# Bilinear field pairs: a third weight tile, field 0 in the weight ring, and stores of four pairs instead of three

## The chip, the cores and the metric

One core of a Trainium2 chip runs the kernel. The metric is device time in microseconds (us) of one execution. The kernel before took 762.01 us (median of three runs, 761.2 to 763.02). The profiled execution took 760.73 us, of which its trace spans 758.7 us from the first to the last instruction. The granted TensorE clock was 0.985 on the mean.

## The reference

There are 32 fields. Each has a vector of 128 numbers for each of 1024 examples. For every pair of fields (i, j) with i < j, 496 pairs in all, the vector of field i goes through that pair's own 128x128 matrix and is then multiplied, element by element, with the vector of field j:

```python
I_IDX, J_IDX = all (i, j) with i < j          # 496 pairs
v_i = inputs[:, I_IDX, :]                     # 1024 x 496 x 128, float32
v_j = inputs[:, J_IDX, :]
transformed = jnp.einsum('bpd,ped->bpe', v_i, W)   # W: 496 x 128 x 128
return transformed * v_j                      # 1024 x 496 x 128, float32
```

The inputs are 16.8 MB of fields and 32.5 MB of matrices; the output is 260 MB. That the output is five times the input is what shapes this kernel.

## The kernel before

**Layout.** The 128 output features lie on the 128 partitions, the 1024 examples along the free axis. One pair of one example set is thus a tile of 128 x 1024 float32: 4 KB in each partition, 512 KB in all. A pair is worked in two halves of 512 examples; `u` counts these halves (0 to 991) and `q = u // 2` counts pairs. The pairs are taken from the last row of i to the first: i = 30 has one pair, i = 0 has 31 (q = 465 to 495), so a field is needed as i for the first time long after the kernel began.

**Arithmetic of a half.** The first 15 pairs (`nq0`) multiply the raw float32 matrix with the raw field (L159). All later ones use a split: ScalarE makes a rounded high part `wh` of two matrices (L95), GpSimd makes `wl` and `wd` from it (L96 to L98); a field is split in the same way into `xh`, `xl`, `xd` (L110 to L116, some of the last step on VectorE, L203). TensorE then does two matmuls into a PSUM bank (L162), ScalarE scales the bank in place (L163), TensorE adds a third (L171), and VectorE multiplies the bank with field j into the output tile `ot` (L177). `first(u)` does the first part, `second(u - LAG)` the rest, three halves later.

**Order.** The schedule is manual: each engine works in the order in which the loop at L186 writes its instructions down. ScalarE's order also holds the issues of most loads, and SyncE's order holds the stores.

**Loads of weights.** Eight matrices come at a time (`WL`, 512 KB, rows of 4 KB). The tiles come from a ring `rpool` of `WB` = 2 tiles. `w_at` (L142 to L145) says after which pair the load of tile c is issued: q = 8c - 11, that is six pairs ahead of the first split that reads it (q = 8c - 5), and not before the matrices that lay in that ring tile were used.

**Loads of fields.** `load_x` (L72) gives each of the 32 fields a tile of its own, 4 KB in each partition, that stays to the end, because a field serves as j for many pairs. Field 0 is the exception: it is never a j, so its raw values are read by its own split and by nothing else. The loop issues field i - 7 at the first pair of row i.

**Stores.** The output tiles come from a ring `opool` of four tiles of `OG` = 3 pairs (12 KB in each partition). Once three pairs are in a tile, SyncE issues one store of 1.5 MB with rows of 12 KB (L184). The first group and the last pairs go one by one or in halves (L182, L179). A tile can be filled again only when all of its store has landed.

**Start.** SyncE issues weights 0, fields 29 and 28, weights 1 and fields 27 to 24; ScalarE issues fields 30 and 31.

Of the kernel before, what the change touches and what calls it, by code (L numbers as in the profile page):

```python
# [7 lines left out]
F32 = mybir.dt.float32  # L8
# [3 lines left out]
P = 128  # L12
NF = 32
NQ = NF * (NF - 1) // 2
BT = 1024
HB = 512
WC = 2
WL = 8
OG = 3
EPS = 2.0**-12  # L20
NATIVE = 5
SHARED = 10
XDLAG = 10
LAG = 3
WB = 2
WLEAD = 6
XLEAD = 5


def _pairs():  # L30

    return [(i, j) for i in range(NF - 2, -1, -1) for j in range(i + 1, NF)]


@with_exitstack
def kernel(
    ctx: ExitStack,
    tc: tile.TileContext,
    xt: bass.AP,
    wt: bass.AP,  # L40
    out: bass.AP,
):

    nc = tc.nc
    pairs = _pairs()  # L60
    nchunk = NQ // WC

    xpool = ctx.enter_context(tc.tile_pool(name="x", bufs=1))
    spool = ctx.enter_context(tc.tile_pool(name="xs", bufs=2))
    rpool = ctx.enter_context(tc.tile_pool(name="wr", bufs=WB))
    wpool = ctx.enter_context(tc.tile_pool(name="ws", bufs=4))
    opool = ctx.enter_context(tc.tile_pool(name="o", bufs=4))
    ppool = ctx.enter_context(tc.tile_pool(name="ps", bufs=8, space=bass.MemoryType.PSUM))

    x_sb = {}  # L70

    def load_x(f, n=1, pieces=1, eng=None):  # L72

        t = xpool.tile([P, n, BT], F32, tag=f"x{f}", name=f"x_{f}")
        s = BT // pieces
        for k in range(pieces):
            (eng or nc.sync).dma_start(out=t[:, :, k * s : (k + 1) * s], in_=xt[:, f : f + n, k * s : (k + 1) * s])
        for k in range(n):
            x_sb[f + k] = t[:, k, :]

    w_raw = {}

    def load_w(c, splits=(0, WL), eng=nc.scalar):
        w_raw[c] = rpool.tile([P, WL, P], F32, tag="w", name=f"w_{c}")
        for a, b in zip(splits, splits[1:]):
            eng.dma_start(out=w_raw[c][:, a:b, :], in_=wt[c, :, a:b, :])

    w_s = {}

    def split_w(c, u):  # L90

        k = c * WC % WL
        raw = w_raw[c * WC // WL][:, k : k + WC, :].rearrange("p q e -> p (q e)")
        h, l, d = [wpool.tile([P, WC * P], F32R, tag=t, name=f"{t}_{c}") for t in ("wh", "wl", "wd")]
        nc.scalar.mul(h, raw, 1.0 - 2.0**-13)  # L95
        nc.gpsimd.tensor_tensor(l, raw, h.bitcast(F32), ALU.subtract)  # L96
        nc.gpsimd.tensor_scalar(d, h.bitcast(F32), EPS, 1.0, ALU.mult, ALU.mult)  # L97
        nc.gpsimd.tensor_tensor(d, l.bitcast(F32), d.bitcast(F32), ALU.subtract)  # L98
        w_s[c] = (h, l, d)

    x_s = {}
    later = []

    def split_x(f, a, u):

        if a == 0:
            x_s[f] = [spool.tile([P, BT], F32R, tag=t, name=f"{t}_{f}") for t in ("xh", "xl", "xd")]
        s = slice(a, a + HB)
        h, l, d = [t[:, s] for t in x_s[f]]
        nc.scalar.mul(h, x_sb[f][:, s], 1.0 - 2.0**-13)  # L110
        nc.gpsimd.tensor_tensor(l, x_sb[f][:, s], h.bitcast(F32), ALU.subtract)  # L111
        nc.gpsimd.tensor_scalar(l, l.bitcast(F32), 1.0 / EPS, 1.0, ALU.mult, ALU.mult)  # L112
        if f > NF - 2 - NATIVE - SHARED:
            later.append((min(u + XDLAG, 2 * first_q[f] + LAG - 1), d, h.bitcast(F32), l.bitcast(F32)))
        else:
            nc.gpsimd.tensor_tensor(d, h.bitcast(F32), l.bitcast(F32), ALU.subtract)  # L116

    nq0 = NATIVE * (NATIVE + 1) // 2
    c0 = nq0 // WC
    first_q = {i: q for q, (i, j) in reversed(list(enumerate(pairs)))}  # L120

    todo = []
    for c in range(c0, nchunk):
        todo.append(((c - 3) * WC + 1, max(c * WC, nq0), lambda u, c=c: split_w(c, u)))
    for i in range(NF - 2 - NATIVE, -1, -1):
        for a in range(0, BT, HB):
            todo.append((first_q[i + 1] + 1 if i < NF - 3 - NATIVE else 2, first_q[i], lambda u, i=i, a=a: split_x(i, a, u)))
    todo.sort(key=lambda t: t[1])  # L130

    load_w(0, (0, 1, WL), nc.sync)
    load_x(NF - 2, pieces=2, eng=nc.scalar)
    load_x(NF - 1, pieces=2, eng=nc.scalar)
    load_x(NF - 3)
    load_x(NF - 4)
    load_w(1, eng=nc.sync)
    for f in range(NF - 5, NF - 4 - XLEAD, -1):
        load_x(f)


    w_at = {}  # L142
    for c in range(WB, -(-NQ // WL)):
        free = (c - WB + 1) * WL if (c - WB) * WL < nq0 else 0
        w_at[max(c * WL - 3 * WC + 1 - WLEAD, free)] = c  # L145


    ctx.enter_context(tc.manual_schedule())
    po, ots = {}, {}


    def first(u):
        q, h = divmod(u, 2)
        i, c = pairs[q][0], q // WC
        r = slice(q % WC * P, (q % WC + 1) * P)
        s = slice(h * HB, (h + 1) * HB)
        po[u] = ppool.tile([P, HB], F32, tag="po", name=f"po_{u}")
        if q < nq0:
            nc.tensor.matmul(po[u], w_raw[q // WL][:, q % WL, :], x_sb[i][:, s], start=True, stop=True)  # L159
        else:  # L160
            for t in (0, 1):
                nc.tensor.matmul(po[u], w_s[c][t][:, r], x_s[i][t][:, s], start=t == 0, stop=t == 1)  # L162
            nc.scalar.mul(po[u], po[u], 1.0 + EPS)  # L163

    def second(u):
        q, h = divmod(u, 2)
        i, j = pairs[q]
        r = slice(q % WC * P, (q % WC + 1) * P)
        s = slice(h * HB, (h + 1) * HB)
        if q >= nq0:  # L170
            nc.tensor.matmul(  # L171
                po[u], w_s[q // WC][2][:, r], x_s[i][2][:, s], start=False, stop=True, skip_group_check=True
            )
        g, k = divmod(q, OG)
        if k == 0 and h == 0:
            ots[g] = opool.tile([P, OG, BT], F32, tag="ot", name=f"ot_{g}")
        nc.vector.tensor_tensor(ots[g][:, k, s], po.pop(u), x_sb[j][:, s], ALU.mult)  # L177
        if q >= NQ - 2:
            nc.sync.dma_start(out=out[g, :, k, s], in_=ots[g][:, k, s])  # L179
        elif g == 0 or q >= NQ - 1 - OG:  # L180
            if h == 1:
                nc.sync.dma_start(out=out[g, :, k], in_=ots[g][:, k])  # L182
        elif k == OG - 1 and h == 1:
            nc.sync.dma_start(out=out[g], in_=ots[g])  # L184

    for u in range(2 * NQ + LAG):  # L186
        q = u // 2
        if u < 2 * NQ:
            i, j = pairs[q]
            if u % 2 == 0 and j == i + 1 and 0 <= i - 2 - XLEAD:  # L190
                load_x(i - 2 - XLEAD, eng=nc.scalar)
            first(u)
            if u % 2 == 1 and q in w_at:
                load_w(w_at[q])
        if u >= LAG:
            second(u - LAG)
        if u % 2 == 1:
            ready = [t for t in todo if t[0] <= q]
            if ready:
                ready[0][2](u)  # L200
                todo.remove(ready[0])
        while later and later[0][0] <= u:
            nc.vector.tensor_tensor(*later.pop(0)[1:], ALU.subtract)  # L203
    assert not todo and not later
# [27 lines left out]
```

## Time and profile before

| What | Value |
|---|---|
| Time, median of 3 runs | 762.01 us |
| Span of the trace | 758.7 us |
| Bytes moved by DMA | 310.07 MB, 409 GB/s over the span |
| of these, HBM written / read | 260.05 / 49.28 MB |
| PE, DVE, ACT, POOL busy | 93%, 84%, 82%, 78% |
| TensorE clock granted, mean | 0.985 |

The engines named are PE (TensorE, matmuls), PEld (its weight loads), DVE (VectorE), ACT (ScalarE), POOL (GpSimd) and SP (SyncE, which issues the stores). "Busy" is the share of the span in which an engine worked. The DMA figures of the profile count packets: one packet is one contiguous row that one of the core's 16 DMA engines moves, or the 4-byte update of a semaphore with which each of the 16 engines ends its part of a transfer. Queue q1 holds what SyncE issued, q10 what ScalarE issued; q8 and q14 carry the program itself.

### The profile page before, as it was taken

The page shows a single profiled execution, that of the slowest core. Times are in us where ns is not written, and L with a number is a line of the kernel's source. Part 1 is how long each engine was busy: PE and PEld are TensorE (multiplying, and loading weights), DVE is VectorE, ACT ScalarE, POOL GpSimd, SP SyncE. Part 2 cuts the span into 40 slices and gives each one's busy share as a digit, 9 for nine tenths or more (in the row PEclk, how much of TensorE's full clock was granted, in tenths as well). Part 3 has the DMA queues.
Part 4 walks back from the last instruction along what each step waited for, and adds up shares of the span by engine and source line. Part 5 has one row for each costly group of instructions (what it writes and reads, how often), then busy time and mean ns, then how long its engine had stood idle before and what let it go on. Part 6 is the DMA issues. An engine that isn't in the chain of part 4 may idle for free.

```text
span 758.7 us, 11264 instructions
## 1 busy us (share of the span) xinstructions
PE 708.1 (93%) x2946; PEld 551.6 (73%) x2946; DVE 633.7 (84%) x1012; ACT 625.7 (82%) x1256; POOL 595.6 (78%) x863
## 2 busy tenths in 40 slices
PE   7979989999999999999998989999999999999992
PEld 3557778777777777777786878778787777777771
DVE  4869989987888779788797989888888888888883
ACT  1368889988888888888887979898899899989881
POOL 0959999999888987978878787888887878786650
PEclk9999999999999999999999999999999999999996
DMA  9999999999999999999999999999999999999996
GB/s 351 427 406 389 425 394 424 427 418 430 420 422 418 425 423 409 419 416 411 400 411 420 404 423 402 422 417 409 410 414 417 402 423 400 408 424 404 416 412 257
DMA packets 38800, 310.07 MB, mean 409 GB/s; under 512 B 4304, under 2 KB 4432, under 8 KB 17872
## 3 DMA queue, kind: packets, MB, share of 16 engines
q1 hardware_dynamic: 26064, 264.25, 83.1%
q10 hardware_dynamic: 12672, 45.09, 16.0%
q8 instruction: 24, 0.39, 0.2%
q14 instruction: 40, 0.33, 0.1%
HBM read 49.28 MB, written 260.05 MB: 408 GB/s over the span
## 4 chain that ended last, share of the span: by engine, by line
DMA 40%; PE 39%; DVE 12%; POOL 5%; issue 1%; ACT 1%; DVEq 0%; ACTq 0%; POOLq 0%
DMA out_dram<-ot 34%; PE po L162 24%; DVE ot L177 12%; PE po L171 12%; DMA w<-in_wt_dram 6%; PE po L159 4%; POOL xl L111 1%; POOL xd L116 1%; POOL wl L96 1%; POOL xl L112 1%; POOL wd L98 1%; ACT po L163 0%; DMA x<-in_xt_dram 0%; DVE xd L203 0%; POOL wd L97 0%
## 5 line engine op out<-in xcount | busy, mean ns | idle before, releaser
L177 DVE TENSOR_TENSOR ot<-po,x 128x512 f32<-128x512 f32 x992 | 619.8, 683 | 109.4 <-DMA out_dram<-ot 46.6
L163 ACT ACTIVATE po<-po 128x512 f32<-128x512 f32 x962 | 540.7, 582 | 58.6 <-PE po L162 24.4
L162 PE MATMUL po<-xh,wh 128*128 128x512 f32 x962 | 382.6, 398 | 13.6 <-DVE ot L177 12.9
L171 PE MATMUL po<-xd,wd 128*128 128x512 f32 x962 | 377.8, 393 | 12.6 <-ACT po L163 11.4
L162 PE MATMUL po<-xl,wl 128*128 128x512 f32 x962 | 378.7, 394 | 5.6 <-POOL wl L96 5.3
L96 POOL TENSOR_TENSOR wl<-w,wh 128x256 fp32r<-128x256 f32 x241 | 181.0, 751 | 76.0 <-ACT wh L95 62.2
L162 PEld LDWEIGHTS po<-xh,wh 128*128 128x128 f32 x962 | 181.8, 189 | 72.0 <-DVE ot L177 33.9
L171 PEld LDWEIGHTS po<-xd,wd 128*128 128x128 f32 x962 | 181.7, 189 | 54.0 <-POOL wd L97 5.7
L162 PEld LDWEIGHTS po<-xl,wl 128*128 128x128 f32 x962 | 182.0, 189 | 46.3 <-POOL wl L96 9.7
L98 POOL TENSOR_TENSOR wd<-wl,wd 128x256 fp32r<-128x256 f32 x241 | 178.4, 740 | 20.1
L95 ACT ACTIVATE wh<-w 128x256 fp32r<-128x256 f32 x241 | 99.8, 415 | 42.3 <-DMA w<-in_wt_dram 38.7
L97 POOL TENSOR_SCALAR wd<-wh 128x256 fp32r<-128x256 f32 x241 | 99.3, 412 | 20.3
L111 POOL TENSOR_TENSOR xl<-x,xh 128x512 fp32r<-128x512 f32 x52 | 69.2, 1331 | 18.6 <-ACT xh L110 18.3
L116 POOL TENSOR_TENSOR xd<-xh,xl 128x512 fp32r<-128x512 f32 x32 | 41.3, 1291 | 2.7
L110 ACT ACTIVATE xh<-x 128x512 fp32r<-128x512 f32 x52 | 32.6, 631 | 12.6 <-DMA x<-in_xt_dram 12.6
L112 POOL TENSOR_SCALAR xl<-xl 128x512 fp32r<-128x512 f32 x52 | 33.3, 641 | 4.6
L159 PE MATMUL po<-x,w 128*128 128x512 f32 x60 | 28.3, 634 | 4.5 <-DMA x<-in_xt_dram 4.5
L159 PEld LDWEIGHTS po<-x,w 128*128 128x128 f32 x60 | 11.8, 202 | 20.2 <-issue 13.0
L203 DVE TENSOR_TENSOR xd<-xh,xl 128x512 fp32r<-128x512 f32 x20 | 16.8, 838 | 3.6 <-POOL xl L112 3.6
L110 ACT ACT_TABLE_LOAD x1 | 1.3, 1283 | 4.6 <-DMA w<-in_wt_dram 4.6
L219 POOL MEMSET const-float32-0.0<- 128x1 f32 x1 | 0.1, 98 | 0.2 <-issue 0.2
L219 POOL MEMSET const-bfloat16-1.0<- 128x1 bf16 x1 | 0.1, 101 | 0.0
(2 smaller groups left out, 0.2 us busy)
## 6 DMA issues: line engine op xcount, KB each, us to landing
out_dram<-ot SPq DMA_DIRECT2D x163, 1536.0 KB, 13.5
w<-in_wt_dram ACTq DMA_DIRECT2D x60, 512.0 KB, 9.0
x<-in_xt_dram ACTq DMA_DIRECT2D x24, 512.0 KB, 9.4
x<-in_xt_dram SPq DMA_DIRECT2D x6, 512.0 KB, 8.5
out_dram<-ot SPq DMA_DIRECT2D x5, 512.0 KB, 11.0
x<-in_xt_dram ACTq DMA_DIRECT2D x4, 256.0 KB, 5.9
out_dram<-ot SPq DMA_DIRECT2D x4, 256.0 KB, 10.1
w<-in_wt_dram SPq DMA_DIRECT2D x1, 512.0 KB, 7.9
```

The source lines that it names most:

```text
L95: nc.scalar.mul(h, raw, 1.0 - 2.0**-13)
L96: nc.gpsimd.tensor_tensor(l, raw, h.bitcast(F32), ALU.subtract)
L97: nc.gpsimd.tensor_scalar(d, h.bitcast(F32), EPS, 1.0, ALU.mult, ALU.mult)
L98: nc.gpsimd.tensor_tensor(d, l.bitcast(F32), d.bitcast(F32), ALU.subtract)
L111: nc.gpsimd.tensor_tensor(l, x_sb[f][:, s], h.bitcast(F32), ALU.subtract)
L112: nc.gpsimd.tensor_scalar(l, l.bitcast(F32), 1.0 / EPS, 1.0, ALU.mult, ALU.mult)
L116: nc.gpsimd.tensor_tensor(d, h.bitcast(F32), l.bitcast(F32), ALU.subtract)
L159: nc.tensor.matmul(po[u], w_raw[q // WL][:, q % WL, :], x_sb[i][:, s], start=True, stop=True)
L162: nc.tensor.matmul(po[u], w_s[c][t][:, r], x_s[i][t][:, s], start=t == 0, stop=t == 1)
L163: nc.scalar.mul(po[u], po[u], 1.0 + EPS)
L171: nc.tensor.matmul(po[u], w_s[q // WC][2][:, r], x_s[i][2][:, s], start=False, stop=True, skip_group_check=True)
L177: nc.vector.tensor_tensor(ots[g][:, k, s], po.pop(u), x_sb[j][:, s], ALU.mult)
```

## The change

Three edits go together, and they keep the memory in each partition the same. The output ring goes from four tiles of three pairs (4 x 12 KB) to three tiles of four pairs (3 x 16 KB), and the stores with it: rows of 16 KB, 2 MB each. The weight ring gets a third tile (+4 KB), and field 0 gives up its own tile (-4 KB): it passes through the weight ring, between weights 54 and 55.

With three weight tiles a load can be issued earlier: q = 8c - 17, twelve pairs ahead of the first split. For tiles 55, 56 and 57, whose ring places stand behind field 0, it stays at 8c - 11. Field 0 is issued by ScalarE after pair 8 x 54 - 11 = 421; the first pair that uses it is q = 465, its split comes soon after q = 436. Weights 2 are now loaded at the start by SyncE, behind field 24, instead of by ScalarE after pair 8.

The purpose is fewer and longer rows in the stores, and weights that are there before they are asked for.

```diff
-OG = 3
+OG = 4
-WB = 2
-WLEAD = 6
+WB = 3
+WLEAD = 12
+XAFTER = 54
...
-    opool = ctx.enter_context(tc.tile_pool(name="o", bufs=4))
+    opool = ctx.enter_context(tc.tile_pool(name="o", bufs=3))
...
-        t = xpool.tile([P, n, BT], F32, tag=f"x{f}", name=f"x_{f}")
+        if f == 0:
+
+            t = rpool.tile([P, WL, P], F32, tag="w", name="x_0").rearrange("p q e -> p (q e)").unsqueeze(1)
+        else:
+            t = xpool.tile([P, n, BT], F32, tag=f"x{f}", name=f"x_{f}")
...
+    load_w(2, eng=nc.sync)
...
         free = (c - WB + 1) * WL if (c - WB) * WL < nq0 else 0
-        w_at[max(c * WL - 3 * WC + 1 - WLEAD, free)] = c
+        early = 0 if XAFTER < c <= XAFTER + WB else WLEAD - 6
+        w_at[max(c * WL - 3 * WC - 5 - early, free)] = c
+    x_at = XAFTER * WL - 11
...
-        elif g == 0 or q >= NQ - 1 - OG:
+        elif g == 0 or q >= NQ - OG:
...
-            if u % 2 == 0 and j == i + 1 and 0 <= i - 2 - XLEAD:
+            if u % 2 == 0 and j == i + 1 and 0 < i - 2 - XLEAD:
                 load_x(i - 2 - XLEAD, eng=nc.scalar)
             first(u)
             if u % 2 == 1 and q in w_at:
                 load_w(w_at[q])
+            if u == 2 * x_at + 1:
+                load_x(0, eng=nc.scalar)
```

## The prediction

> **What bounds the kernel now.** I read the page's DMA lines first, then the waits, then short stretches of the DMA view.
>
> ```profile
> DMA  9999999999999999999999999999999999999996
> ...
> DMA packets 38800, 310.07 MB, mean 409 GB/s; under 512 B 4304, under 2 KB 4432, under 8 KB 17872
> ...
> q1 hardware_dynamic: 26064, 264.25, 83.1%
> q10 hardware_dynamic: 12672, 45.09, 16.0%
> ```
>
> The 16 DMA engines are at nine tenths or more in 39 of 40 slices, and the queues' shares add up to over 99% of the span. PE (93%) and DVE (84%) leave more room. The waits agree:
>
> ```profile
> DVE ot L177 <- DMA out_dram<-ot: 46.6, 49, 1.4
> ACT wh L95 <- DMA w<-in_wt_dram: 38.7, 39, 9.1
> ```
>
> VectorE, the last engine of the pipeline, waits 49 times for an output tile whose store hasn't landed: compute is ahead of the DMA, not behind it. ScalarE's 38.7 us for weights looks as large, but costs time only where it lets the DMA engines run dry.
>
> How fast is a saturated engine? A stretch with almost nothing but 12 KB stores (724 to 734 us), and one with nothing but 4 KB rows (8 to 12 us):
>
> ```profile
> q1 hardware_dynamic: 378, 4.21, 99.2%
> ```
> ```profile
> DMA packets 443, 1.64 MB, mean 411 GB/s; under 512 B 37, under 2 KB 37, under 8 KB 443
> ```
>
> In the first, 0.992 x 16 x 10 us over 342 big packets (4.21 MB / 12,288 B) is about 464 ns each. In the second, all queues fill 64 engine-us with 406 rows: 158 ns each. The packet records give cleaner medians: 460 ns for 12,288 B, 159 ns for 4,096 B, 84 ns for 2,048 B. The slope is 301 ns / 8,192 B = 0.03674 ns/B, and what is left at zero bytes is 8.5 ns. A packet starts about 4 ns before its predecessor on the same engine ends, so the real fixed cost is 4 to 5 ns: a 12 KB row occupies an engine for 456 ns, a 4 KB row 155 ns.
>
> The end shows a second thing (752.9 to 757.4 us):
>
> ```profile
> q1 hardware_dynamic: 49, 0.11, 6.2%
> ```
>
> 6.2% of 16 engines is one engine. Fifteen have finished by 752.9 us (most by 751.5), and **one straggler** works alone until 757.3. The semaphore landings show the same lag long before: from about 300 us on, most stores land on their last engine 4 to 6.6 us after the fifteenth. An output tile comes free only when the straggler is done, so the end is set by the straggler's own sum of packets.
>
> The chain of waits shows the rhythm:
>
> ```profile
> 587.82 3.69 DVE ot L177 x6
> 591.53 12.92 DMA out_dram<-ot
> 604.57 3.69 DVE ot L177 x6
> 608.28 13.81 DMA out_dram<-ot
> ```
>
> When a tile comes free, VectorE fills it in 3.69 us (0.615 us a half), and the store lands 13 to 14 us after its issue because it stands behind others.
>
> [...] 12,288 B in 456 ns on 16 engines is 431 GB/s[...]. The new stores have a pitch of 16 KB; the field loads here have 128 KB and run at 159 to 164 ns a row. [...]
>
> **The change, part by part.**
>
> *Longer rows.* Before, each engine stores 163 x 8 rows of 12 KB, 5 x 8 of 4 KB and 32 of 2 KB. After: pairs 0 to 3, 492 and 493 singly, 494 and 495 in halves, and 488 pairs in 122 stores. A 16 KB row by the slope: 456 + 4,096 x 0.03674 = 606.5 ns. Work of one engine: before 1,304 x 0.456 + 40 x 0.155 = 600.8 us; after 976 x 0.6065 + 48 x 0.155 = 599.4 us. **Saved 1.4 us.** DMAs fall from 269 to 229; 40 semaphore updates of about 6 ns save 0.2 us. With the uncorrected 460 and 610.5 ns the sum would be 3.1 us, the upper bound; the lower bound is nothing, should the overlap hide the whole fixed cost. I take 1.6 us. All of it lies on the straggler's path, hence on the end. No 16 KB store exists in this trace: the only 16 KB packets, 24 of the program's on q8, took 953 ns at the median, but [...] program packets of 8 KB on q14 keep to the slope (309 ns).
>
> *Weights twelve pairs ahead.* Six pairs at 1.53 us (759 us / 496) are 9.2 us, just the 9.0 us in which a load lands, hence the 39 waits. Twelve are 18.4 us; with 16 KB store rows between its packets a load should land in 10 to 11 us, so nearly all of the 38.7 us goes. Most of it was hidden by the store backlog. What shows in the DMA is the stall at 39 to 45 us: ScalarE waits 5.8 us for weights, its scalings stand behind that wait, VectorE waits 5.1 us for the third matmul, and once the backlog is used up fewer than 8 engines move anything from 53.9 to 54.7 us. Weights 2 are now there from the start and weights 3 are issued eight pairs earlier. **Saved 0.8 us** (0 to 1.5).
>
> *Weights 55 to 57* keep six pairs and may wait 1 to 2 us each; behind that wait are ScalarE's scalings, then TensorE and VectorE, with 8 or so pairs of stores queued. Costed at nothing. *Field 0* is loaded 15 pairs (23 us) before its split: nothing. *Weights 2 at the start* put 512 KB (1.2 us) before the first stores, but the same bytes leave later slices: nothing.
>
> *Three output tiles instead of four.* When the straggler lands a tile, it still has two tiles queued: 16 x 0.6065 = 9.7 us (before: 24 x 0.456 = 10.9). VectorE needs 8 x 0.615 = 4.9 us (before 3.7), and about 1.3 us pass from an issue to its first packet, as at the start. The straggler is thus refilled 3.5 us before it is dry (before 5.9): no cost. But that margin is also how far the other fifteen can run ahead: 5.9 us explains the 4 to 6.6 us seen. It should fall to about 3.5, the fifteen idling more while the straggler goes on.
>
> Sum: 762.0 - 1.6 - 0.8 = 759.6; I say **759.5**.
>
> **The rivals.**
>
> *A, forecast: 759.5.*
>
> *B, nothing measurable: 761.3.* The fixed cost is mostly overlapped, and the early hole moves elsewhere instead of closing. For it: the early hole is one event, and the straggler sets the end. Some 0.7 us remain.
>
> *C, slower: 766.* Coarser stores starve the DMA engines. For it: from 48 to 110 us stores are issued with only one or two others outstanding, and their first engine lands them 5 to 8 us later, of which 3.65 us is the store itself: the backlog is 1.3 to 4.4 us. A fourth pair delays an issue by two halves at TensorE's pace (6 matmuls, 0.23 us apart), 1.36 us. Losing 0.3 us on each of 15 stores there makes 4.5 us. If the straggler isn't one engine but whichever was stalled last, the shorter margin hurts later too: 2.4 us less, lost once. Less the 1.6 saved, about 766 at the worst. Against it: the backlog is thin there because of the weight stalls, which go.
>
> *D, better: 757.* The mean store packet takes 7 ns above the median. If such stalls come per packet and not per byte, 5,248 packets fewer save 5,248 x 7 / 16 = 2.3 us more. Against it: stalls of about 500 ns strike several engines at once, like an event in time.
>
> **How the numbers follow.** A 0.45, B 0.22, C 0.18, D 0.15. Faster A + D 0.60, same B, slower C. The lower end, 756.3, takes in D with a little run-to-run spread; the upper end, 764.8, takes in B and the milder half of C.
>
> **What would show it.** Packets on q1 at 20,448 instead of 26,064; the median 16 KB row at 610 ns (above 620 the first step is wrong); ScalarE's wait for weights under 8 us; no hole near 54 us; a straggler alone at the end for 3 to 4 us rather than 5.8. Wrong, if all engines show idle time between 50 and 130 us, or store rows take over 1.34 times the old ones.

## The result

The changed kernel took 756.49 us (median of six runs, 756.21 to 756.93), the one before 761.69 us (six runs, 760.32 to 763.02): a ratio of 0.9932, 95% interval 0.992 to 0.9945. It is 5.2 us faster. The forecast was 759.5 us, the range 756.3 to 764.8. One execution of an experiment below (996.08 us at a granted clock of 0.656, its neighbours 0.97 to 0.99) was in a slow state and is left out of its median.

The DMA lines of the changed kernel's page, and two of its waits:

```profile
DMA  9999999999999999999999999999999999999997
...
DMA packets 33039, 310.06 MB, mean 411 GB/s; under 512 B 3664, under 2 KB 3792, under 8 KB 17360
...
q1 hardware_dynamic: 20448, 264.77, 84.2%
q10 hardware_dynamic: 12528, 44.57, 15.3%
```

```profile
DVE ot L186 <- DMA out_dram<-ot: 55.6, 55, 2.1
...
ACT wh L100 <- DMA w<-in_wt_dram: 3.9, 3, 1.5
```

The same bytes go in 5,761 fewer packets, and the DMA engines are as full as before. VectorE still waits for output tiles (55.6 us, before 46.6): compute is still ahead of the DMA. (L186 is the line that was L177 before, L100 was L95.) ScalarE's wait for weights fell from 38.7 us in 39 waits to 3.9 us in 3. In the packet records a 16 KB row has a median of 611 ns.

The straggler at the end, 750.2 to 753.3 us:

```profile
q1 hardware_dynamic: 50, 0.09, 7.7%
```

7.7% of 16 engines is 1.2 engines, so again one is nearly alone, but for 3.2 us instead of 5.6. The chain of waits has the same rhythm as before, with fills of eight halves:

```profile
510.83 4.88 DVE ot L186 x8
515.74 11.65 DMA out_dram<-ot
527.51 4.88 DVE ot L186 x8
532.41 12.61 DMA out_dram<-ot
```

Where the time went can be summed up from the packet records of the two traces: for the mean engine, the packets of q1 and q10 at their median duration (in both traces a packet starts 3 to 4 ns before its predecessor ends; 4 ns are taken off), what these packets took beyond it, and idle time. The trace before spans 758.7 us, the one after 754.7.

| us of the mean DMA engine | before | after |
|---|---|---|
| rows at their median, semaphores included | 721.4 | 720.2 |
| beyond the median | 21.5 | 21.8 |
| idle, 20 to 100 us | 0.94 | 0.07 |
| idle, 100 us until the first engine is done | 3.5 | 3.6 |
| idle while the straggler finishes | 5.4 | 3.1 |

1.2 us come from the rows, 0.9 from the start, 2.3 from the end, less 0.3 beyond the median and 0.1 idle in between. That is bookkeeping, not yet cause: the straggler is never idle at the end, so it must have had less work or been held up less before, and the table doesn't say which.

### The profile page after: what moved, and what is told of

It is laid out like the page before. It is cut to its first block, busy times and chain, and to the rows that moved or that the text cites. A ratio compares the mean times of both kernels' runs of the same rounds, so it can differ in the third digit from the quotient of the medians.

```text
span 754.7 us, 11212 instructions
## 1 busy us (share of the span) xinstructions
PE 707.8 (94%) x2946; PEld 546.5 (72%) x2946; DVE 622.9 (83%) x1012; ACT 632.2 (84%) x1256; POOL 596.8 (79%) x863
## 4 chain that ended last, share of the span: by engine, by line
DMA 56%; DVE 24%; PE 14%; POOL 3%; issue 1%; ACT 0%; DVEq 0%; ACTq 0%; SPq 0%; POOLq 0%
DMA out_dram<-ot 53%; DVE ot L186 24%; PE po L171 10%; PE po L180 5%; DMA x<-in_xt_dram 2%; POOL xl L116 1%; POOL xd L121 1%; POOL xl L117 0%; DVE xd L214 0%; POOL wl L101 0%; ACT po L172 0%; DVEq L186 0%; POOL wd L103 0%; ACTq L82 0%; POOL wd L102 0%
## 5 line engine op out<-in xcount | busy, mean ns | idle before, releaser
L186 DVE TENSOR_TENSOR ot<-po,x 128x512 f32<-128x512 f32 x992 | 610.7, 681 | 117.7 <-DMA out_dram<-ot 55.6
L172 ACT ACTIVATE po<-po 128x512 f32<-128x512 f32 x962 | 547.6, 583 | 87.1 <-PE po L171 30.9
L101 POOL TENSOR_TENSOR wl<-w,wh 128x256 fp32r<-128x256 f32 x241 | 179.1, 743 | 72.8 <-ACT wh L100 71.4
L103 POOL TENSOR_TENSOR wd<-wl,wd 128x256 fp32r<-128x256 f32 x241 | 181.3, 752 | 20.1
L100 ACT ACTIVATE wh<-w 128x256 fp32r<-128x256 f32 x241 | 99.3, 412 | 5.7 <-DMA w<-in_wt_dram 3.9
L214 DVE TENSOR_TENSOR xd<-xh,xl 128x512 fp32r<-128x512 f32 x20 | 15.1, 753 | 3.2 <-POOL xl L117 3.2
## 6 DMA issues: line engine op xcount, KB each, us to landing
w<-in_wt_dram ACTq DMA_DIRECT2D x59, 512.0 KB, 10.4
out_dram<-ot SPq DMA_DIRECT2D x6, 512.0 KB, 10.4
```

## The experiments

**Each part alone.** First the stores' part with the weights as before, and the weights' part with the stores as before:

```diff
# e1_stores_only, from the kernel before
-OG = 3
+OG = 4
-    opool = ctx.enter_context(tc.tile_pool(name="o", bufs=4))
+    opool = ctx.enter_context(tc.tile_pool(name="o", bufs=3))
-        elif g == 0 or q >= NQ - 1 - OG:
+        elif g == 0 or q >= NQ - OG:
# e2_weights_only, from the changed kernel: the same three edits undone
```

> The stores' part alone: four pairs in 16 KB rows from three tiles; weights and field 0 as before. Theory (two parts that add: shorter fixed cost of rows on the slowest DMA engine, and the early weights): 1.6 us faster than before, about 760.1 us, the lag of the slowest engine at the end near 3.6 us. Rival 1 (it is the ring that lets the other engines run less far ahead, which takes load off the slowest one): 4 us faster, about 757.7 us. Rival 2 (coarser stores need the early weights, or the DMA engines run dry after the early stall): no faster than before, or slower by 1 to 3 us, with a hole of idle DMA engines near 54 us longer than the 0.8 us of before.

> The weights' part alone: third weight tile, field 0 in that ring, loads twelve pairs ahead; stores of three pairs from four tiles as before. Theory: 2.7 to 3.5 us faster, 758.2 to 759 us, with all of the gain in the first 100 us, and the lag at the end still 5 to 6 us. Rival 1 (the ring): under 1 us faster. As forecast in the prediction: 0.8 us faster, 760.9 us.

Measured: the stores' part alone 768.3 us (seven executions, 764.39 to 773.42) against 761.18 us for the kernel before on the same chip, ratio 1.009 (1.0055 to 1.0125), **slower by about 7 us**. The weights' part alone 758.3 us, ratio 0.9963 (0.9949 to 0.9977), 2.9 us faster. The parts do not add. The waits of the stores' part alone show what goes wrong:

```profile
ACT wh L95 <- DMA w<-in_wt_dram: 65.6, 34, 6.8
DVE ot L177 <- PE po L171: 57.2, 53, 6.3
...
DVE ot L177 <- DMA out_dram<-ot: 3.3, 3, 1.4
```

Beside 16 KB store rows a weight load lands in 9.9 us (median) instead of 9.0, later than the six pairs (9.2 us) that it has. That difference alone is weak, for two traces of the weights' part alone have 9.6 and 8.9 us; the row experiments below make it firmer. ScalarE's wait grows from 38.7 to 65.6 us. VectorE now waits for the third matmul (57.2 us) and hardly ever for an output tile (3.3 us, before 46.6): compute has fallen behind the DMA. Rival 2 was right, and the loss is larger than it gave.

The windows show where. Columns: stretch, its length, busy us of PE, its weight loads, DVE, ACT and POOL with instruction counts, TensorE clock, DMA share, GB/s. The kernel before, the weights' part alone (as run again below, c2) and the stores' part alone:

```profile
20.00:60.00 40.00, 34.90 (x119) 23.14 (x117) 30.88 (x49) 21.49 (x46) 30.26 (x40) 0.96 1.00 410
60.00:100.00 40.00, 36.67 (x150) 28.37 (x151) 38.08 (x58) 32.96 (x68) 36.90 (x50) 0.97 1.01 415
100.00:140.00 40.00, 40.00 (x176) 32.93 (x175) 39.33 (x63) 36.89 (x77) 36.53 (x53) 0.99 1.00 410
```

```profile
20.00:60.00 40.00, 38.67 (x144) 26.75 (x143) 36.43 (x58) 25.92 (x55) 35.66 (x48) 1.00 1.02 427
60.00:100.00 40.00, 37.25 (x159) 29.10 (x158) 35.34 (x58) 35.21 (x73) 36.90 (x51) 1.00 1.01 427
100.00:140.00 40.00, 37.81 (x156) 28.46 (x156) 34.42 (x58) 34.13 (x70) 35.84 (x50) 1.00 1.01 425
```

```profile
20.00:60.00 40.00, 34.23 (x113) 22.94 (x112) 28.84 (x45) 19.71 (x41) 29.07 (x39) 0.91 0.92 387
...
100.00:140.00 40.00, 38.39 (x156) 31.24 (x157) 35.97 (x56) 35.00 (x73) 33.71 (x48) 0.91 0.92 373
```

Read the last column. With early weights the DMA moves 425 to 427 GB/s from 20 to 140 us, before 410 to 415. That is 17 + 12 + 15 GB/s over 40 us each, 1.8 MB, or 4.1 us of DMA time; 0.5 MB of it is a weight tile that is merely fetched sooner, so by estimate about 2.9 us are won, which is what the measured times show. A DMA share of 1.00 in the kernel before hides most of this. Its slow stretches are 40 to 60, 60 to 80 and 100 to 120 us (393, 403 and 392 GB/s); in the last two the engines were idle for 2% at most, but their rows took longer (load rows 174 and 193 ns on the mean, 160 with early weights). What lengthens the rows is not shown. The stores' part alone drops to a share of 0.92.

The clock column shows something that neither the prediction nor the expectations had. In the trace before, TensorE stands still for 4.8 us from 41.5 us on, behind the wait for weights, and then it is granted half its clock for 3.4 us:

```profile
46.40:49.80 3.40, 3.40 (x9) 2.65 (x9) 1.79 (x3) 2.77 (x7) 2.85 (x5) 0.50 1.00 394
```

The same happens at 97.6 us, after a standstill of 2.3 us; the stores' part alone has 6.8 us of it at 46.0 and again at 100.6 us. With early weights the clock is 1.00 in all three stretches. So late weights cost TensorE these standstills (4.8 and 2.3 us) and then time at the lower clock; no run separates the two, and none shows what lowers the clock.

The higher rate lies in the start alone. Later the weights' part alone is no faster than the kernel before (first line before, second c2). Both stay below 427 GB/s, though in c2 the weights' splits wait for loads no more than 0.5 us in all:

```profile
180.00:400.00 220.00, 209.28 (x884) 163.21 (x883) 180.21 (x294) 192.69 (x386) 186.13 (x269) 1.00 1.01 416
180.00:400.00 220.00, 209.01 (x881) 162.14 (x880) 179.57 (x294) 192.22 (x383) 186.32 (x270) 1.00 1.01 415
```

The changed kernel is the same 1.8 MB ahead at 140 us, but loses part of that lead from 140 to 180 us (first line before, second c1, the changed kernel run again below), and is 0.6 MB ahead at 740 us:

```profile
140.00:180.00 40.00, 39.11 (x167) 30.51 (x166) 35.37 (x56) 35.28 (x74) 36.90 (x53) 1.00 1.01 423
140.00:180.00 40.00, 37.66 (x158) 28.89 (x157) 34.28 (x57) 34.62 (x71) 33.12 (x48) 1.00 1.00 401
```

That need not be lost time. Its other fifteen engines end 2.4 us less far ahead of the straggler, by estimate 0.9 MB that the mean rate misses and the straggler does not.

**Which of the weight loads counts.** From the weights' part alone, weights 7 and later go back to six pairs ahead:

```diff
# e5_early_weights_only, from e2_weights_only
-        early = 0 if XAFTER < c <= XAFTER + WB else WLEAD - 6
+        early = 0 if c > 6 else WLEAD - 6
```

> As the weights' part alone, but only weights 2 to 6 are loaded early; from weights 7 on the load is issued six pairs ahead again, as before. Theory (only the start gains): the same time as with all weights early, within 0.7 us. Rival 2b (the 39 short waits for weights all along cost time): the gain of the weights' part shrinks to less than half.

Measured 758.81 us, ratio 0.9975 (0.9963 to 0.9987): by the ratios 1.9 us of the 2.8. The waits for weights in its trace are above those of the kernel before:

```profile
ACT wh L100 <- DMA w<-in_wt_dram: 51.3, 37, 5.4
```

The trace is not of a typical execution: it took 762.23 us, the second longest of 22, and in it TensorE stood still for 4.4 us at 403 us and then had half its clock for 6.8 us. What 51 us of waiting cost can thus not be read from the median. At the median the late weights behind number 6 cost about 0.5 us, and the intervals overlap; but 6 of the 22 executions took over 760 us, against 2 of 16 with all weights early. With the old stores, the early weights at the start carry most of the gain.

**The ring, apart from the rows.**

```diff
# e3_three_tiles_of_three, from the kernel before
# e9_weights_three_of_three, from e2_weights_only
-    opool = ctx.enter_context(tc.tile_pool(name="o", bufs=4))
+    opool = ctx.enter_context(tc.tile_pool(name="o", bufs=3))
# e8_two_tiles_of_four, from the changed kernel: bufs=3 to bufs=2
```

> The kernel before with three output tiles of three pairs instead of four (36 KB instead of 48). The refill margin worked out as in the prediction is 16 x 0.456 - 3.7 - 1.3 = 2.3 us, still positive. Theory: the slowest engine stays fed, time within 1 us of before, except that the early stall of weights leaves a longer hole (up to 2 us slower); lag at the end 2 to 3 us. Rival 1 (less running ahead is what helps): 2 us faster than before. Rival of the other kind (backlog matters all along): 5 us slower or more.

> The weights' part with three output tiles of three pairs (36 KB) instead of four. It has neither the longer rows nor the deeper ring. Theory (the stores' part gains by its rows alone, 1.4 to 2.4 us): the same as the weights' part alone, 758.4 us within 1 us; the slowest engine is alone at the end for about 2 us instead of 5.5, and the others idle that much more before. Rival (a shorter ring, which keeps the engines closer together, is itself a gain): 1.5 to 2.5 us faster than the weights' part alone, 756.5 us. Other rival (a ring of nine pairs is too small even with early weights): over 2 us slower than the weights' part alone.

> The changed kernel with two output tiles of four pairs (32 KB) instead of three. When a store lands only one other is queued, 8 x 0.6065 = 4.85 us, and the refill takes 4.9 + 1.3 = 6.2 us. Theory of the refill margin: short by 1.35 us at each of 122 stores; the load rows of the same stretch (0.85 us a store and engine) fill part of it. Slower by 60 to 165 us, 816 to 920 us. Rival (the margin does not matter, work queues elsewhere): within 10 us of the changed kernel.

Measured: e3 761.82 us, ratio 0.9998 (0.9981 to 1.0015); e9 758.39 us, ratio 0.996 (0.9946 to 0.9975), the same as with four tiles. e9's straggler is alone for 1.9 us at the end instead of 5.6, without a gain. So a shorter run-ahead of the other engines is worth nothing by itself, and neither is the fourth tile. e3 also clears one suspect in e1: three tiles instead of four cost nothing even with late weights, so e1's 7 us come with its stores of four pairs. Whether they come by the longer rows or by the later issue of each store was not separated. e8 took 844.33 us, ratio 1.107 (1.1039 to 1.1101): 88 us more than the changed kernel, 0.72 us a store, inside the 60 to 165 us expected. Its VectorE waits:

```profile
DVE ot L186 <- DMA out_dram<-ot: 158.5, 79, 5.5
```

The refill margin (rows still queued when a tile comes free, less fill and issue) tells these apart: with early weights, margins of 5.9, 2.3 and 3.5 us (c2, e9, the changed kernel) show no cost, and -1.35 us costs 88 us.

**What a row costs.** Unused bytes inside the output tile cut the same 2 MB stores into shorter rows:

```diff
# e4_rows_4k, from the changed kernel
-            ots[g] = opool.tile([P, OG, BT], F32, tag="ot", name=f"ot_{g}")
+            ots[g] = opool.tile([P, OG, BT + 4], F32, tag="ot", name=f"ot_{g}")
-            nc.sync.dma_start(out=out[g], in_=ots[g])
+            nc.sync.dma_start(out=out[g], in_=ots[g][:, :, :BT])
# e7_rows_8k: the same, 16 bytes in the middle of the tile, rows of 8 KB
```

> The changed kernel, with 16 unused bytes between the four pairs of an output tile, so that the same 2 MB stores from the same three tiles go out in rows of 4 KB. Fixed cost per row of 4 to 5 ns: a pair's row costs 155.3 ns instead of 606.5 / 4 = 151.6, so 3.7 ns x 4 x 976 = 14.3 us more on every DMA engine: 756.5 + 14.3 = 770.8 us. Rival (the fixed cost is hidden by the overlap of packets): within 3 us of the changed kernel, so no slower than before.

> The changed kernel with 16 unused bytes in the middle of each output tile, so that its stores go out in rows of 8 KB instead of 16. The packets' fixed cost in full: 4.8 ns x 976 = 4.7 us slower than the changed kernel. Half of it, as with the 4 KB rows: 2.3 us slower. Nothing: rows of 8 KB and more are alike, and the gain of the stores' part has another cause.

The DMA lines of the two show that the rows were cut (the 4 KB rows first):

```profile
DMA packets 79887, 310.06 MB, mean 407 GB/s; under 512 B 3664, under 2 KB 3792, under 8 KB 79824
```

```profile
DMA packets 48655, 310.06 MB, mean 410 GB/s; under 512 B 3664, under 2 KB 3792, under 8 KB 17360
```

Measured: 4 KB rows 763.09 us, ratio to the kernel before 1.0028 (1.0019 to 1.0038), 6.6 us above the changed kernel. By the medians, 4 x 155 - 607 = 13 ns on each of 976 rows, it should have been 12.7 us. 8 KB rows took 757.99 us (0.9963, 0.9951 to 0.9974), 1.6 us above the changed kernel on the same chip (756.42); by their median of 309 ns, 2 x 305 - 607 = 3 ns, it should have been 2.9 us. Both times about half arrives; for the 8 KB rows that is rough, since durations are recorded in whole ns and the 3 ns may be anything from 1.5 to 4.5. In both traces part of the rest is visible: load rows, which move beside the stores, are shorter. With 4 KB rows they take 161.7 ns on the mean instead of 167.8, 6.1 ns x 10,624 / 16 = 4.1 us less for each engine; with 8 KB rows 164.6 instead of 168.7 (c1), 2.7 us less. A whole weight load also lands sooner: in 7.8, 8.2 and 10.4 us beside rows of 4, 8 and 16 KB, where nothing else differs. Why the load rows get shorter is not shown, and the length of the store rows is not all of it: beside the 12 KB rows of the kernel before they take 175.6 ns.

**The changed kernel beside the weights' part alone, on one chip.**

> The changed kernel itself, on the same chip as the three beside it, so that their differences are free of the spread between chips. From the runs so far: 4.5 to 5.5 us faster than before.

> The weights' part alone, on the same chip as the changed kernel: how much the stores' part adds once the weights are early. Rows by their fixed cost as the packets show it: the changed kernel is 1.4 us faster than this. Rows at half of it, as the 4 KB rows suggest (14.1 us by the packets, 6.6 measured): 0.7 us. The runs so far: 1.9 us.

Measured 756.42 us (756.03 to 757.31; ratio 0.9944, 0.9931 to 0.9957) and 758.12 us (757.76 to 758.3; ratio 0.9965, 0.9954 to 0.9977). Once the weights are early, **the stores' part adds 1.7 us**. At half of the packets' fixed cost the rows give 0.7 us of it, by estimate. The packet records of these two traces don't confirm the share: from c2 to c1 the rows at their median lose 1.1 us, the time beyond the median grows by 3.4 and idle time falls by 3.5, 2.2 of that at the end.

The other 1 us might come from 40 DMAs fewer. That was to be told by issuing each store in two:

```diff
# e10_store_halves, from the changed kernel
-            nc.sync.dma_start(out=out[g], in_=ots[g])
+            for a in (0, 64):
+                nc.sync.dma_start(out=out[g, a : a + 64], in_=ots[g][a : a + 64])
```

> The changed kernel with each 2 MB store issued as two of 64 partitions (1 MB each): same 16 KB rows, same tiles, 122 more store DMAs. If the stores' part gains because there are 40 fewer DMAs (beyond the 6 ns of each semaphore update): this loses three times what the stores' part gained, 3 us or more. If it gains by rows alone: 122 x 6 ns, 0.7 us slower than the changed kernel.

Measured 921.79 us, ratio 1.2125 (1.2089 to 1.216). The test doesn't answer its question, for it changed something far larger. Its DMA line:

```profile
DMA packets 34993, 310.08 MB, mean 338 GB/s; under 512 B 5616, under 2 KB 5744, under 8 KB 19312
```

The number of rows is right, and their median is still 611 ns, but their mean is 772 ns instead of 626.

**A better lead behind field 0.**

```diff
# e6_lead_behind_field0, from the changed kernel
-        early = 0 if XAFTER < c <= XAFTER + WB else WLEAD - 6
+        early = 2 if XAFTER < c <= XAFTER + WB else WLEAD - 6
```

> The changed kernel with weights 55 to 57 issued eight pairs ahead (8c - 13) instead of six. In the changed kernel ScalarE waits 3.9 us for these three and the DMA engines idle 16 engine-us (1.0 us each) between 660 and 680 us. Theory: the hole closes, 0.5 to 1 us faster than the changed kernel, about 755.7 us. Rival (the hole is hidden behind the slowest engine, which had work): no change, 756.5 us.

Measured 756.52 us (755.98 to 756.77), ratio 0.9936 (0.9921 to 0.995): no change. The hole between 660 and 680 us is gone from its trace (16 engine-us of idle in the changed kernel, under 1.5 here), and so is the wait for weights; the time is the same. No run here was clearly faster than the changed kernel.

## Why the prediction was right, and where it was off

**Direction and bound: right.** The DMA engines bound both kernels (q1 and q10 fill 99% of the span in each); both of case A's gains showed in experiments, and the measured time lies inside the range, near its lower end. The gain was 5.2 us where 2.5 was forecast.

**Weights twelve pairs ahead: the mis-sized term.** Forecast 0.8 us (0 to 1.5), measured 2.7 to 2.9 us (e2, c2). The mechanism was right: the wait fell to 3.9 us, and a load landed in 10.4 us (median), inside the 10 to 11 that the author had estimated. The start counts most (e5), but the term was sized from the one hole in which fewer than 8 engines moved anything. Three stretches between 40 and 120 us ran at 392 to 403 GB/s, two of them with hardly an idle engine. That these were the ones to be won shows only beside the run with early weights: later slices of the same GB/s row are as low (400 to 404), and early weights don't raise them. The halved clock behind the stall (3.4 us from 46.4 us on) was not in the account either.

**Longer rows: 1.6 forecast, 1.7 measured for the whole stores' part.** The agreement is partly luck. The fixed cost of 4 to 5 ns is in the packets' durations, and the median row came at 611 ns as forecast, but only about half of it reaches the end (6.6 of 12.7 us in e4, 1.6 of 2.9 in e7), so the rows give by estimate 0.7 us. What gives the other 1 us stays open. It is not the shorter ring by itself (e9); whether it is the smaller number of DMAs could not be separated.

**Three tiles at no cost: right with the weights' edit; without it the coarser stores cost 7 us.** The margin of 3.5 us held, e8 shows what a negative one costs, and the straggler's lag fell to 3.2 us as forecast. But the costing was done for the edits together. Rival C's mechanism, compute too late for coarser stores, is what e1 shows at 7 us; the argument against it, that the weight stalls go, is what kept it away. The chief virtue of the weights' part is that it makes the stores' part possible.

**Weights 55 to 57 and field 0: right.** They do leave waits (3.9 us) and a hole of 1 us, and removing both changes nothing (e6).

**Rival D:** store packets did not lose their excess with their number. It went from 7 ns on 20,864 rows to 15 ns on 15,616, 9.4 and 14.9 us an engine, while the load rows lost 5.2 us an engine (175.6 to 167.8 ns). All packets together took 21.5 us an engine beyond their medians before and 21.8 after, and 17.6 with four times as many store rows (e4). Stalls did not go with the number of packets, as was argued against D.

**Sums that don't hold.** The upper bound of 3.1 us for the rows is 3.0 by its own figures, and rival C's terms add up to 767.3 us, not 766; neither moves the forecast.

The two medians taken together give 5.2 us, the parts 2.8 + 1.7 = 4.5 us; the 0.7 us between is no more than the spread of the kernel before (its medians were 760.8 to 761.7 us), so no third cause need be looked for in it.

## What to carry to other kernels

Two edits that look independent can be one. Here a load landed later beside longer store rows (7.8 us with 4 KB, 10.4 with 16 KB), so a prefetch lead that just covers a load's landing time has to grow before the stores do (e1: a lead of 9.2 us, a landing in 9.9, 7 us lost). At a DMA bound, don't size a stall from idle engines alone, since busy engines can take longer over each row (at 60 to 80 and 100 to 120 us load rows took 174 and 193 ns on the mean, with early weights 160); take the bytes moved in that stretch with and without the stall. The best stretch of the kernel is too high a mark: after 180 us this kernel kept to 411 to 416 GB/s even where weights were hardly ever waited for. In these runs a ring of store tiles was deep enough when what was queued as a tile came free outlasted its refill (margins of 2.3 to 5.9 us against -1.35, which cost 88 us), and depth beyond that bought nothing (e9 758.39 us, c2 758.12).

## What the runs showed of the hardware

With each store issued as two halves of 64 partitions (e10) the DMA moved 338 GB/s over the span, with stores of 128 partitions 411, in the same number of 16 KB rows. Each half has 16 semaphore updates, as many as a whole store (1,952 more on q1 for 122 more stores). Six of ten rows still take 611 to 624 ns; a second peak lies at 1,260 to 1,280 ns, about twice the median. What lengthens these rows was not shown.

In e4 and e7 shorter rows cost about half of what the packets' own durations say (6.6 of 12.7 us, 1.6 of 2.9 us), while the load rows beside them got shorter by 4.1 and 2.7 us an engine.

A 512 KB weight load landed in 7.8, 8.2 and 10.4 us (medians of e4, e7 and the changed kernel) beside store rows of 4, 8 and 16 KB. Beside 4 KB rows (e4) a load row followed directly on something of the store queue nine times in ten; in the kernel before, beside 12 KB rows, only about half of the time, and most of the others followed on another load row. (Packet records name no engine; successors were matched by the end of one and the start of the next.)

TensorE's granted clock fell to one half for 3.4 us at 46.4, 97.6 and 408.2 us in the trace before, each time within 1.4 us of the end of a standstill (4.8, 2.3 and 1.9 us). A standstill of 2.5 us at 441.3 us had no such sequel, so these traces give no rule for it.
